# Graph attention on one core: the sender rows of four quads loaded row by row by SyncE instead of gathered by GpSimd

## The chip, the core and the metric

One core of a Trainium2 chip runs the whole kernel. The metric is the device time of one execution in microseconds, taken as the median of several runs; before the change it is 2042.45 us (three runs, 2042.1 to 2043.92). A profile of one further execution comes with it.

The engines are PE (TensorE; PEld is its loading of weights), DVE (VectorE), ACT (ScalarE), POOL (GpSimd) and SP (SyncE). SP computes nothing here; it issues DMAs and waits for semaphores.

## What is computed

There are N = 6250 nodes with 128 features `x`, and E = 206250 edges, sorted by receiver. Each edge has two vectors of 32 features, a weight, a sender and a receiver. Cut to what matters:

```python
w = silu(e1 @ rad_W1 + rad_b1) @ rad_W2 + rad_b2 + silu(e2 @ sph_W1 + sph_b1) @ sph_W2 + sph_b2
q = (x @ Wq)[dst];  k = (x @ Wk)[src];  v = (x @ Wv)[src]       # 8 heads of 16
alpha = (q * w * k).sum(head) / sqrt(16) * weight[:, None]
out = layernorm(x + segment_sum(alpha * v, dst, N) / 16)
```

So each edge needs one row of 256 numbers (k and v of its sender, 1 KB) from a table of all nodes. The senders come in no order.

## The kernel before

**Tiling.** 128 edges make a tile, four tiles a quad (512 edges, `QT = 4`), four quads a group. There are 403 quads and 101 groups; the last group has three quads. Everything is issued in an order written out by hand; no scheduler moves it.

**Head.** The kernel computes k and v for all nodes and stores them as `kv_tab` in DRAM (lines 223 to 236, 338 to 355). The senders of all edges are loaded to `src_i`, one column of 128 numbers for each tile. For the first ten quads (`XQ`) rows of `x` are gathered instead and k and v computed from them. Then come the gathers of four more quads (line 356), the sum of biases and the bias rows (358, 359), and the turning of the receivers on PE (360).

**Main loop** (lines 603 to 671). A step is a *slot*: one quad, taken in each group in the order 0, 2, 1, 3. The list `order` holds the quads in that order, and slot i works on `order[i]`. In a slot:

- PE computes the first layer of the quad two ahead (line 408), the queries at the edges of the quad one ahead (419), and that quad's second layer (455).
- ACT applies silu (440).
- DVE multiplies query and key of the quad one ahead (462, the first use of the quad's row of k and v), then by the edge's weight vector (469), sums the heads (471), and makes the message (484).
- PE adds the messages of the previous group by products with one-hot tables (495, 529).
- POOL gathers the rows of k and v for the quad 14 ahead (`AHEAD = RING - 2`): `gathers` makes a tile `kv` from a ring of 16 and issues four indirect DMAs, each of 128 rows (line 120). Each of them waits for one product of line 455 (its `marks`), so that no gather runs ahead of TensorE.
- SP loads, each once in a group, the window of `x` three groups ahead (`load_x`, lines 162 and 165; its address comes from a register loaded from `gb_i`), the features two groups ahead (142, 512 KB) and the receivers two groups ahead (153), and writes at most one finished window of rows in a slot (`write_rows`, 561). The loads of `x` and of the features wait for a product of TensorE.

The queues are in order: what SP is told in a slot waits until SP has issued all that stands before it.

After the loop the last quad is done in two halves, and the last rows are written (710). A general path for other receivers (lines 715 to 826) isn't taken.

Of the kernel before, what the change touches and what calls it, by code (L numbers as in the profile page):

```python
# [12 lines left out]
F32 = mybir.dt.float32  # L13
BF16 = mybir.dt.bfloat16
U8 = mybir.dt.uint8
I32 = mybir.dt.int32
AF = mybir.ActivationFunctionType
OP = mybir.AluOpType
# [3 lines left out]
SP = mybir.EngineType.SP  # L22
WAIT = mybir.DependencyInfo(mybir.DependencyClass.Sync, mybir.DependencyReason.DATA)

P = 128
N = 6250
D = 128
# [5 lines left out]
QT = 4  # L33
# [4 lines left out]
EQ = P * QT  # L38
# [3 lines left out]
ROWS = (NB + 1) * P  # L42
W = 32
LB = 4
XQ = 10
RING = 16
CHECK = 20
XL = 3
NEIGHBORS = 16.0
# [5 lines left out]
def gnn_kernel(ctx, tc, x, src, dst, weight, edges, rad_W1, rad_b1, rad_W2, rad_b2,  # L55
# [14 lines left out]
    nc = tc.nc  # L70
    const = ctx.enter_context(tc.tile_pool(name="const", bufs=1))
    dram = ctx.enter_context(tc.tile_pool(name="dram", bufs=1, space=DRAM))

    kv_tab = dram.tile([NB * P, 2 * D], F32, name="kv_tab")
# [5 lines left out]
    dst_i = const.tile([P, NT], I32, name="dst_i")  # L80
    src_i = const.tile([P, NT], I32, name="src_i")
    src_x = const.tile([P, math.ceil(XQ / NQ) * GT], I32, name="src_x")
    scale = const.tile([P, NT], F32, name="scale")
    w1 = const.tile([P, D], F32, name="w1")
    w2 = const.tile([P, 2, D], F32, name="w2")
# [5 lines left out]
    ident = const.tile([P, P], F32, name="ident")  # L91
# [24 lines left out]
    def quad_of(name, bufs, width=D):  # L116
        return ep.tile([P, QT, width], F32, name=name, bufs=bufs)

    def gather(o, table, index):
        return nc.gpsimd.indirect_dma_start(  # L120
            out=o, out_offset=None, in_=table,
            in_offset=bass.IndirectOffsetOnAxis(ap=index, axis=0))

    order = [g * NQ + j for g in range(NG) for j in (0, 2, 1, 3) if g * NQ + j < QUADS]
    r_of = {}
    feats_of, relb_of, act_of, kv_of, hot_of, hotT_of, x_of, q_of, msg_of = ({} for _ in range(9))
    po_of, part_of, to_of, tot_of, xT_of, y0_of, kq_of, pick_of, pq_of, pw_of = ({} for _ in range(10))

    def gathers(q, marks=()):

        kv = quad_of("kv", RING, 2 * D)
        for t in range(QT):
            o = gather(kv[:, t, :], kv_tab, src_i[:, q * QT + t:q * QT + t + 1])
            if marks:
                tc.add_manual_dep(o.ins, marks[t].ins.name, WAIT, reason="no gather ahead of TensorE")
        kv_of[q] = kv

    def load_feats(g, mark=None):  # L140
        feats_of[g] = gp.tile([P, EG // 2], F32, name="feats")
        o = nc.sync.dma_start(feats_of[g], edges[g])
        if mark is not None:
            tc.add_manual_dep(o.ins, mark.ins.name, WAIT, reason="one signal of TensorE a quad")
# [27 lines left out]

    nc.sync.dma_start(src_x, src[:, :math.ceil(XQ / NQ) * GT])
    nc.scalar.dma_start(wkv[:, :D], Wk)
# [12 lines left out]
    with tc.tile_pool(name="nodes", bufs=1) as nodes, \  # L187
            tc.tile_pool(name="nodes_ps", bufs=2, space=PSUM) as nps:
        chunks = [(c, min(QT, NB - c)) for c in range(0, NB, QT)]
        quads_x = order[:XQ]  # L190
        xs_of = {}
# [19 lines left out]
        def gather_x(q):  # L211
            xs_of[q, "x"] = xs = quad_of("msg", XQ)
            for t in range(QT):
                gather(xs[:, t, :], x, src_x[:, q * QT + t:q * QT + t + 1])
# [8 lines left out]
        def k_and_v(k, n):  # L223
            kvs = quad_of("kv", RING, 2 * D)
            for h in range(0, n, 2):
                m = min(2, n - h)
                pk = nps.tile([P, 2, 2 * D], F32, name="pk", bufs=3)
                for i in range(m):
                    nc.tensor.matmul(pk[:, i, :], xT_of[k][:, h + i, :], wkv, start=True, stop=True)
                nc.vector.tensor_copy(kvs[:, h:h + m, :], pk[:, :m, :])  # L230
            return kvs
# [88 lines left out]

        AHEAD = RING - 2
        beside = {3: [firsts], 4: [starts], 5: [lambda: receivers(0)], 6: [tables],
# [15 lines left out]
        for i, (k, n) in enumerate(work):  # L338
# [15 lines left out]
            if i == len(chunks) - 1:  # L354
                nc.sync.dma_start(scale, weight)
        for q in order[XQ:AHEAD]:
            gathers(q)
        nc.vector.tensor_tensor(bsum, b2[:, 0:1], b2[:, 1:2], op=OP.add)
        bias_rows()
        for t in range(P, NT, P):  # L360
# [5 lines left out]
    with tc.tile_pool(name="ps", bufs=1, space=PSUM) as pp:  # L366
# [113 lines left out]
        def messages(q, alpha, t=slice(0, QT), marks=()):  # L480

            if t.start == 0:
                msg_of[q] = quad_of("msg", XQ)
            o = nc.vector.tensor_tensor(  # L484
# [50 lines left out]
        def statistics(g):  # L535
            first = g // LB * LB if g < NG - 3 else g
            if g == first:
                y0_of[g] = (gp.tile([P, LB, D], F32, name="y0"), gp.tile([P, LB, 2], F32, name="mv"))
            y0, mv = y0_of[first]
# [4 lines left out]
            nc.vector.bn_aggr(mv[:, k - 1, :], st)  # L544
            if k == LB or g >= NG - 4:
                sd = gp.tile([P, LB], F32, name="sd")
                nc.scalar.activation(sd[:, :k], mv[:, :k, 1], AF.Sqrt, bias=eps)
                rs = gp.tile([P, LB], F32, name="rs")
                nc.vector.reciprocal(rs[:, :k], sd[:, :k])
                shift = gp.tile([P, LB], F32, name="shift")  # L550
                nc.vector.scalar_tensor_tensor(shift[:, :k], mv[:, :k, 0], -1.0, rs[:, :k],
# [6 lines left out]
        def write_rows(n=1):  # L558
            for _ in range(min(n, len(written))):
                g, y = written.pop(0)  # L560
                nc.sync.dma_start(rows_from(out, r_of.pop(g)), y.bitcast(U8))
# [41 lines left out]
        for g in range(NG):  # L603
            last = g == NG - 1
            for slot, j in enumerate((0, 2, 1, 3)):
                q = g * NQ + j
                i = g * NQ + slot
                if q >= QUADS:
                    continue
                turned, past, old = None, mark, marks  # L610
                if slot == 0 and g == CHECK + len(checks) + 1:
                    verdict()
                if slot == 0 and g + 1 < NG:
                    turned = turn_q(g + 1)
                if slot == 1 and 2 <= g:
                    turned = sum_group(g - 2)
                if slot == 2 and g + 1 < NG:
                    turned = make_q(g + 1)
                if 1 <= g:
                    for t in ((), (0, 1), (2, 3))[slot] if last else ((), (0, 1), (2,), (3,))[slot]:  # L620
                        mark = sum_quads(g - 1, t)
                if last and slot == 2:
                    po_of[g] = pp.tile([P, EQ], F32, name="ph", bufs=2)[:, :D]
                    for t in range(QT):
                        sum_wide(order[i - 2], t, start=(t == 0))
                if i + 2 < len(order):
                    first_layers(order[i + 2])
                if i + 1 < len(order):
                    mark = q_at_edges(order[i + 1])
                    marks = weigh(order[i + 1])  # L630
                if i + 2 < len(order):
                    silus(order[i + 2], mark, marks)
                if turned:
                    turned()
                if 1 <= g and slot == 3:
                    part_sums(g - 1)
                if i + AHEAD < len(order):
                    gathers(order[i + AHEAD], old[-QT:])
                if i + 1 < len(order):
                    multiply(order[i + 1], mark)  # L640
                    messages(q, scores(q, marks=marks), marks=marks)
                if slot == 0:
                    if g + XL < NG:
                        load_x(g + XL, past)
                if slot == 2 and g + 2 < NG:
                    load_feats(g + 2, past)
                    load_rel(g + 2)
                if slot == 1:
                    if g + 1 < NG:
                        one_hots_T(g + 1)  # L650
                    if g + 2 < NG:
                        pick(g + 2)
                    if 1 <= g < NG - 1:
                        place(g - 1)
                    if last:
                        wide_one_hots(g * NQ + 1)
                        place(g)
                        n = nc.values_load(general, min_val=0, max_val=1)
                if last and slot == 0:
                    wide_one_hots(g * NQ + 2)  # L660
                    place(g - 1)
                write_rows()
                if slot == (2 if last else 3) and 2 <= g:
                    statistics(g - 2)
                if slot == 3:
                    if g + 1 < NG - 1:
                        one_hots(g + 1)
                    if g + 1 == NG - 1:
                        wide_one_hots((g + 1) * NQ)
                    if CHECK <= g < CHECK + len(checks):  # L670
                        checks[g - CHECK]()
        g, q = NG - 1, order[-1]
# [18 lines left out]
        for t in range(QT // 2):  # L691
# [5 lines left out]
                                       op0=OP.mult, op1=OP.mult)  # L697
# [171 lines left out]
```

## Time and profile before

| | |
|---|---|
| median of 3 runs | 2042.45 us |
| profiled execution, its own time | 2043.99 us |
| its span, first to last instruction | 2042.2 us |
| mean granted clock of TensorE | 0.922 |
| PE busy / its weight loads | 90% / 75% of the span |
| DVE, ACT, POOL busy | 72%, 35%, 75% |
| DMA | 304 MB, 149 GB/s; mean share of the 16 DMA engines some 0.50 |
| queue of POOL's gathers | 76736 packets, 208.77 MB, 36.1% of 16 engines |
| queue of SP | 62912 packets, 92.00 MB, 13.8% |

The busy time of an engine counts its instructions alone. SP's instructions (register moves, semaphore waits, the issue of DMAs) don't count as busy, so its load is read from the duration and count of each kind. A group's line names the line of the kernel, the engine and operation, what is written from what, the count, then busy time in us and mean ns, and the idle time before it with what ended most of it. A wait is written as who waited, for whom, the sum in us, how often, and the longest.

### The profile page before, as it was taken

To read this page: it belongs to the slowest core of one execution; us is meant where nothing else is said; L and a number is where in the kernel's file an instruction comes from. 1 tells how busy PE (TensorE), PEld (TensorE's weight loads), DVE (VectorE), ACT (ScalarE), POOL (GpSimd) and SP (SyncE) were. 2 spreads that over 40 slices of the span, in tenths; PEclk is the share of its full clock that TensorE was granted. 3 is DMA by queue.
4 is the path that set the end of the run, shared out by engine and by line. 5 is a ranking of instruction groups with operands and counts; after the bars stand their busy time and mean duration, and the time that the engine had idled before them with its cause. 6 is when DMAs were issued, how large, how long until landed. Compare 5 with 4: busy or idle time off the path is not lost.

```text
span 2042.2 us, 44162 instructions
## 1 busy us (share of the span) xinstructions
PE 1843.1 (90%) x16011; PEld 1527.2 (75%) x16011; DVE 1466.9 (72%) x3005; ACT 720.1 (35%) x1425; POOL 1529.6 (75%) x1620
## 2 busy tenths in 40 slices
PE   9999998889899999898999989898998999898987
PEld 7788887777777777777777777777776777777776
DVE  6698887677767677677767667776766767677766
ACT  2334443333333323333333333233333333333333
POOL 7777777777777777777777777777777777777774
PEclk9899999899898898899888988998989989989889
DMA  8555554545445544545454554445454544544452
GB/s 309 149 150 154 154 157 145 153 136 152 140 147 141 153 146 142 146 143 152 136 151 142 149 148 145 146 142 148 140 152 136 153 140 148 151 143 147 140 149 81
DMA packets 141371, 304.03 MB, mean 149 GB/s; under 512 B 34028, under 2 KB 73820, under 8 KB 141148
## 3 DMA queue, kind: packets, MB, share of 16 engines
q0 software_dynamic: 76736, 208.77, 36.1%
q1 hardware_dynamic: 62912, 92.00, 13.8%
q8 instruction: 127, 2.08, 0.4%
q14 instruction: 96, 0.79, 0.1%
q10 hardware_dynamic: 1500, 0.40, 0.1%
HBM read 287.58 MB, written 13.46 MB: 147 GB/s over the span
## 4 chain that ended last, share of the span: by engine, by line
PE 50%; DMA 19%; DVE 14%; issue 7%; ACT 4%; POOL 4%; DVEq 0%; POOLq 0%; ACTq 0%
PE pw L455 24%; DMA kv<-kv_tab,src_i 19%; PE pq L419 10%; PE ph L408 7%; DVE kq L462 5%; PE po L495 4%; DVE side L471 2%; DVE kq L469 2%; PE pw L450 2%; POOL kv L120 2%; POOL msg L120 2%; ACT y L554 2%; ACT L440 2%; PE pq L388 1%; PE pq L529 1%
## 5 line engine op out<-in xcount | busy, mean ns | idle before, releaser
L120 POOL DMA_INDIRECT kv<-kv_tab,src_i x1572 | 1489.9, 948 | 479.7 <-issue 188.9
L440 ACT ACTIVATE act<-ph,b 128x512 f32<-128x512 f32 x806 | 518.7, 685 | 1176.6 <-PE pq L419 1149.0
L455 PE MATMUL pw<-w,act 128*128 128x128 f32 x6448 | 911.1, 300 | 0.1
L455 PEld LDWEIGHTS pw<-w,act 128*128 128x128 f32 x6448 | 830.1, 208 | 105.5 <-issue 93.2
L462 DVE TENSOR_TENSOR kq<-pq,kv 128x512 f32<-128x512 f32 x403 | 277.6, 689 | 401.6 <-DMA kv<-kv_tab,src_i 225.1
L419 PE MATMUL pq<-q,hotT 32*128 32x128 f32 x3224 | 498.1, 297 | 29.6 <-DVE kq L462 28.8
L408 PE MATMUL ph<-feats,w 32*128 32x512 f32 x1612 | 502.6, 681 | 23.3 <-ACT act L440 23.3
L419 PEld LDWEIGHTS pq<-q,hotT 32*128 32x128 f32 x3224 | 419.2, 199 | 87.0 <-issue 57.7
L471 DVE TENSOR_REDUCE side<-kq 128x32 f32<-128x512 f32 x404 | 279.9, 693 | 41.6
L484 DVE TENSOR_TENSOR msg<-kv,side 128x512 f32<-128x512 f32 x404 | 277.3, 686 | 43.4 <-DVE side L473 1.2
L469 DVE TENSOR_TENSOR kq<-pw,kq 128x512 f32<-128x512 f32 x404 | 274.1, 678 | 0.0
L408 PEld LDWEIGHTS ph<-feats,w 32*128 32x128 f32 x1612 | 137.6, 193 | 106.4 <-issue 59.6
L450 PE MATMUL pw<-brow,onesb 3*128 3x512 bf16 x403 | 161.1, 400 | 1.1 <-DVE kq L469 1.1
L495 PE MATMUL po<-msg,hot 128*32 128x128 f32 x3200 | 155.8, 292 | 0.0
L529 PE MATMUL pq<-part,to 128*128 128x128 f32 x200 | 45.6, 311 | 94.4 <-DVE kq L462 62.1
L473 DVE TENSOR_TENSOR side<-side,scale 128x32 f32<-128x32 f32 x404 | 80.6, 199 | 42.2 <-DVE side L471 0.5
L529 PEld LDWEIGHTS pq<-part,to 128*128 128x128 f32 x200 | 30.5, 192 | 106.8 <-issue 63.2
L495 PEld LDWEIGHTS po<-msg,hot 128*32 128x32 f32 x3200 | 71.4, 111 | 38.7 <-issue 5.3
L388 PE MATMUL pq<-wq,xT 128*128 128x128 f32 (+1 forms) x202 | 47.5, 320 | 37.3 <-DVE kq L462 36.9
L394 DVE TENSOR_TENSOR hotT<-relb,side 128x512 f32<-128x512 bf16 x101 | 68.7, 680 | 0.0
L388 PEld LDWEIGHTS pq<-wq,xT 128*128 128x128 f32 (+1 forms) x202 | 34.6, 214 | 45.6 <-DVE kq L462 44.9
L399 DVE TENSOR_TENSOR hot<-rel,side 128x512 f32<-128x512 f32 x100 | 66.1, 661 | 0.0
(107 smaller groups left out, 832.0 us busy)
## 6 DMA issues: line engine op xcount, KB each, us to landing
feats<-in_edges SPq DMA_DIRECT2D x101, 512.0 KB
kv<-kv_tab,src_i POOLq DMA_INDIRECT x1572
relb<-rel_lin SPq DMA_DIRECT2D x101, 128.0 KB
x<-in_x SPq DMA_DIRECT2D x101, 64.0 KB
out<-y SPq DMA_DIRECT2D x101, 64.0 KB
kv_tab<-kv SPq DMA_DIRECT2D x12, 512.0 KB
act<-in_x SPq DMA_DIRECT2D x12, 256.0 KB
dst_i<-in_dst SPq DMA_DIRECT2D x1, 808.0 KB
```

The costliest lines, as they stand in the source:

```text
L120: return nc.gpsimd.indirect_dma_start(out=o, out_offset=None, in_=table, in_offset=bass.IndirectOffsetOnAxis(ap=index, axis=0))
L388: nc.tensor.matmul(pt[:n, :D], xT_of[g][:, :n], wq, start=True, stop=True)
L408: return nc.tensor.matmul(act_of[q, i], w1[r0:r0 + R, :], feats_of[g][r0:r0 + R, c0:c0 + EQ], start=True, stop=True)
L419: o = nc.tensor.matmul(pq_of[q][:, t, :], hotT_of[g][b, t * P:(t + 1) * P], q_of[g][b, :], start=True, stop=True)
L440: o = nc.scalar.activation(act, act_of[q, i], AF.Silu, bias=b1[:, i:i + 1])
L450: nc.tensor.matmul(pw, onesb, brow.rearrange("p t d -> p (t d)"), start=True, stop=False)
L455: o = nc.tensor.matmul(pw[:, t, :], act_of[q, i][:, t * P:(t + 1) * P], w2[:, i, :], start=False, stop=(t == QT - 1 and i == 1))
L462: o = nc.vector.tensor_tensor(kq_of[q], pq_of[q], kv_of[q][:, :, :D], op=OP.mult)
L469: nc.vector.tensor_tensor(m, pw_of[q][:, t, :], m, op=OP.mult)
L471: o = nc.vector.tensor_reduce(alpha, m.rearrange("p t (h e) -> p t h e", e=HD), AX.X, OP.add)
L484: o = nc.vector.tensor_tensor(msg_of[q][:, t, :].rearrange("p t (h e) -> p t h e", e=HD), kv_of[q][:, t, D:].rearrange("p t (h e) -> p t h ...
L495: o = nc.tensor.matmul(po_of[g][j * W:(j + 1) * W, :], hot_of[g][:, j * QT + t, :], msg_of[g * NQ + j][:, t, :], start=(t == 0), stop=(t = ...
```

## The change

Four quads are not gathered any more. With `ROW_LEAD = 8`, `every` is (403 - 8) // 4 = 98, so `row_at` is 98, 196, 294, 392: the quads at these positions of `order`. For them `gathers` returns at once.

Their rows come from SP. `load_rows(i)`, called in every slot after `write_rows`, issues units of 16 edges: one load of 16 addresses into registers of SP, then 16 DMAs, each of one row of 1 KB from `kv_tab` to one partition of a tile `rows` (two buffers). A quad has 32 units. They are spread over the slots since the last such quad's (91 slots for the first, 98 for each other), none or one in a slot, and end eight slots before the quad's own position.

The addresses are made at the head: DVE multiplies the senders of the four quads by 1024, PE turns the 128x16 result, DVE copies it to `at_i` as integers, so that the addresses of one tile lie in one partition.

The change's short description also speaks of small weights on SyncE's queue; the diff has no such edit, and the small weights are still issued by ACT (line 343).

```diff
+ROW_BYTES = 2 * D * 4
+ROW_QUADS = 4
+ROW_LEAD = 8
+ROW_UNIT = 16
...
+    at_i = const.tile([ROW_QUADS * QT, P], I32, name="at_i")
...
+    every = (len(order) - ROW_LEAD) // ROW_QUADS
+    row_at = [(n + 1) * every for n in range(ROW_QUADS)]
+    row_quads = {order[i] for i in row_at}
...
     def gathers(q, marks=()):
 
+        if q in row_quads:
+            return
         kv = quad_of("kv", RING, 2 * D)
...
+    def load_rows(i):
+
+        k = max(i + ROW_LEAD - 1, 0) // every
+        if k >= ROW_QUADS:
+            return
+        q, start = order[row_at[k]], max(k * every - ROW_LEAD + 1, 0)
+        slots, units = row_at[k] - ROW_LEAD + 1 - start, EQ // ROW_UNIT
+        a, b = ((j * units + slots - 1) // slots for j in (i - start, i - start + 1))
+        if i == start:
+            kv_of[q] = quad_of("rows", 2, 2 * D)
+        table = kv_tab.bitcast(U8).rearrange("(o n) b -> o (n b)", o=1)
+        for u in range(a, min(b, units)):
+            t, e = u * ROW_UNIT // P, u * ROW_UNIT % P
+            _, rows = nc.values_load_multi_w_load_instructions(
+                at_i[k * QT + t:k * QT + t + 1, e:e + ROW_UNIT], engines=(SP,), min_val=0,
+                max_val=(N - 1) * ROW_BYTES, skip_runtime_bounds_check_because="senders are nodes")
+            for p in range(ROW_UNIT):
+                nc.sync.dma_start(kv_of[q][e + p:e + p + 1, t, :].bitcast(U8),
+                                  table[:, ds(rows[p], ROW_BYTES)])
...
         for q in order[XQ:AHEAD]:
             gathers(q)
+        rows_f = nodes.tile([P, ROW_QUADS * QT], F32, name="rows_f")
+        for k, i in enumerate(row_at):
+            nc.vector.tensor_scalar(rows_f[:, k * QT:(k + 1) * QT],
+                                    src_i[:, order[i] * QT:(order[i] + 1) * QT],
+                                    float(ROW_BYTES), None, op0=OP.mult)
+        pt = nps.tile([P, QT, P], F32, name="pt", bufs=3)
+        nc.tensor.transpose(pt[:ROW_QUADS * QT, 0, :], rows_f, ident)
+        nc.vector.tensor_copy(at_i, pt[:ROW_QUADS * QT, 0, :])
         nc.vector.tensor_tensor(bsum, b2[:, 0:1], b2[:, 1:2], op=OP.add)
         bias_rows()
...
                 write_rows()
+                load_rows(i)
                 if slot == (2 if last else 3) and 2 <= g:
```

## The prediction

> **What bounds the kernel now.** I read the page's busy times first, then the groups of instructions, the timeline of POOL, the waits, and the count of multiplications (line 462, one for each quad of 512 edges) by stage.
>
> ```profile
> PE 1843.1 (90%) x16011; PEld 1527.2 (75%) x16011; DVE 1466.9 (72%) x3005; ACT 720.1 (35%) x1425; POOL 1529.6 (75%) x1620
> ...
> L120 POOL DMA_INDIRECT kv<-kv_tab,src_i x1572 | 1489.9, 948 | 479.7 <-issue 188.9
> ```
>
> By busy share PE looks like the bound and POOL like an engine with a quarter of its time to spare. The second line takes that back: 1489.9 us busy and 479.7 us idle make 1969.6 us for 1572 gathers, 1.253 us each. POOL's timeline shows what the idle time is:
>
> ```profile
> 2017.20 0.94 POOL L120 DMA_INDIRECT kv<-kv_tab,src_i  x1 [0.30 <-PE pw L455]
> ...
> 2018.45 0.94 POOL L120 DMA_INDIRECT kv<-kv_tab,src_i  x1 [0.30 <-issue]
> ...
> 2019.70 0.95 POOL L120 DMA_INDIRECT kv<-kv_tab,src_i  x1 [0.31 <-issue]
> ...
> 2020.95 0.94 POOL L120 DMA_INDIRECT kv<-kv_tab,src_i  x1 [0.30 <-issue]
> ...
> 2022.20 0.95 POOL L120 DMA_INDIRECT kv<-kv_tab,src_i  x1 [0.31 <-issue]
> ```
>
> The gap is 0.30 us whatever is named as its cause: a fixed step of the instruction, not a wait. From 53.76 us to 2023.15 us POOL gathers without a pause, 4 x 1.253 = 5.01 us a quad. What the others would do, the stages show (length, busy time and count of line 462, then clock, DMA share, GB/s):
>
> ```profile
> 100.00:150.00 50.00, 9.31 (x14) 1.00 0.52 154
> 150.00:200.00 50.00, 8.22 (x12) 0.97 0.54 155
> 200.00:250.00 50.00, 8.23 (x12) 0.97 0.53 154
> 250.00:300.00 50.00, 8.90 (x13) 1.00 0.51 151
> ...
> 600.00:800.00 200.00, 27.57 (x40) 0.88 0.50 146
> ```
>
> While the ring of rows is full (to about 300 us) 51 quads take 200 us, 3.92 us each, with PE 96 to 100% busy; later 40 take 200 us, 5.0 us each, which is POOL's pace. The waits agree: hardly any on a gather's DMA before 300 us, and over the whole span
>
> ```profile
> DVE kq L462 <- DMA kv<-kv_tab,src_i: 225.1, 165, 4.7
> ```
>
> So POOL sets the end: its last gather, then 19.1 us of tail. PE, at 3.9 to 4.2 us a quad, has about a fifth to spare.
>
> **What goes.** Four quads (positions 98, 196, 294 and 392 of 403) lose their four gathers: 16 x 1.253 = 20.05 us off POOL, with nothing beside them. After each of these quads PE and DVE have two quads to do in one 5.01 us gap; at some 4.1 us each they fall 3.2 us behind and recover 0.9 us a quad, four quads later. Even the last has ten quads left for that, so all four count. What is late next is still the next gather.
>
> **What comes at the head.** Four multiplications 128x4, a transpose on PE and a copy stand before the bias rows. Nearest rows: a tensor-scalar 128x4 takes 0.23 us (line 504), and small ones start 0.07 to 0.2 us apart; a transpose 0.34 us (line 307); a copy of 128x128 0.29 us (line 296). That is 0.5 + 0.34 + 0.25 and two hand-overs of about 0.1, or 1.3 us. It isn't hidden: PE's first product of the main loop starts at 65.78 us, after the pick of 65.40 us, which follows the bias rows on DVE; and the first gather that waits for TensorE (75.26 us) stood idle 0.89 us instead of 0.30, so it already waits for that chain. I take 1.3 us, lost once; bounds 0 (another wait covers it) and 2.5 us (each step at its longest row, and the twelve turns of the receivers pushed back behind the new transpose).
>
> **What comes on SP.** 2048 row loads of 1 KB in 128 units: one register load for 16 addresses, then 16 DMAs. The rows nearest to it:
>
> ```profile
> L162 SPq TENSOR_LOAD <-gb_i x101: 269/737/1132, 23.8 to 1944.2; - x101
> ```
>
> ```profile
> L165 SPq MOVE x<-in_x x101: 29/38/39, 24.9 to 1945.1; - x101
> L165 SPq DMA_DIRECT2D x<-in_x x101: 332/339/358, 25.0 to 1952.0; - x101
> L165 SPq EVENT_SEMAPHORE  x97: 17/17/28, 68.5 to 1945.0; - x97
> ```
>
> A DMA whose address is in a register costs 0.339 + 0.038 + 0.017 = 0.394 us of SP, 16 of them 6.3 us (8.8 us if back to back they take 0.497, the longest of line 205's loads of x). The load of 16 registers isn't in the trace: 0.74 us if it costs what one register does, 11.8 us if it costs 16 times the median. I take 16 times the fastest, 0.269, so 4.3 us, as consecutive reads should not each bear the median's full delay. A unit is then 10.6 us, with ends at 7.0 and 20.6.
>
> The Trainium skill ("Runtime: NRT & Kernel Launch", "What's in a NEFF") puts a register load at about 200 ns a register even in bulk; by that estimate the load is 3.2 us, the unit 9.5 us, and the sum stays what it is.
>
> The units lie on slots 0 to 384, one in 3.01 slots (2.84 for the first quad), that is 14.2 to 15.1 us at POOL's pace. SP's own work in four slots is 0.74 + 0.34 (x) + 0.34 (features) + 0.57 (receivers) + 0.34 (rows out) + 0.1 = 2.43 us, so 1.8 us in that stretch. This leaves 12.5 us or more for a unit of 10.6: SP is filled to about 85%, and its present waits for PE (over 1300 us in all) cover it. Behind a unit on SP stand the features and receivers of two groups ahead and the rows out. They come up to 10.6 us later than now, and have about four slots, 20 us, less some 5 us to land. The rows themselves must be there seven slots (35 us) after the last unit.
>
> SP also waits for older DMAs, because their signals are shared:
>
> ```profile
> SPq L334 <- DMA wkv<-in_Wv: 0.6, 1, 0.6
> ```
>
> That load has no data in common with the one named. Between them stand seven other loads from SP and ACT, so I read eight signals in turn: a row waits until the eighth DMA before it has landed. A gather lands 1.92 us after POOL has written it (ended 2013.13, used 2015.05), and eight rows take 3.2 us to issue, so it costs nothing, unless a landing takes over 3.2 us, as behind a 512 KB feature load (the rows out wait for the one before up to 5.7 us). DVE's multiplication of such a quad must see up to eight signals: well under 1 us, in an engine 72% busy.
>
> **The sum.** 20.05 - 1.3 = 18.75 us off. The profiled execution took 2043.99 us (span 2042.2), 1.54 us over the median of 2042.45; it would become 2025.2, and the median 2023.7. Everything else I cost at nothing: the 2 MB travel either way, the tail is the same.
>
> **Rivals.**
> 1. *Part is given back* (2029.9 us). The two quads in one gap are not caught up after the last of the four (PE's clock falls to 0.86 in some stretches): 5.0 us lost, and the head costs 2.5: 2042.45 - 20.05 + 7.5. For it: line 455 at times takes 3.71 us for 16 products instead of 2.05. Against it: ten quads remain.
> 2. *SP becomes the bound* (slower). It decides once a unit takes over 12.5 us, which with 6.3 us of DMAs is a register load over 6.2 us, 0.39 us a register. Then features arrive late for every group, and SP's order paces the loop. At 0.50 us a register (the register loads of line 658 take 0.46 to 0.54) a unit is 14.3 us: 70 us head, 128 x 14.3 + 96 x 2.43 = 2064, 18 quads at 5.0 and 16 us tail make 2240 us; at the median 0.737 it is 2730. For it: only single loads are seen, and their median is above the limit. Against it: one instruction for 16 neighbouring words should not pay 16 times.
> 3. *No gain* (2043.7 us). The transfers, not POOL's writing of descriptors, pace the gathers; then it is the same who issues them, and the head's 1.3 us remain. For it: 19% of the chain of waits is put down to the gathers' DMA. Against it: a DMA share of 0.50 in every stage, and POOL's even steps. The Trainium skill ("DMA: Bandwidth & Descriptors", "Issuing engines are not separate DMA queues") states this rule: all queues run on the same 16 engines, and another issuing engine saves only the sequencer's time to initiate, usually small. By it the change would be worth nothing; the trace has that time as 1.253 us a gather on the path, so here it is not small.
>
> **How the numbers follow.** Forecast 70%, rival 1 12%, rival 2 14%, rival 3 4%. The forecast's own spread is 2020.5 (head 0, and POOL's few long gathers, up to 1.82 us, fewer) to 2027. The range 2020.5 to 2034 takes in the forecast and rival 1 (82%). What a measurement tells from no change is about 0.2%, 4.1 us: faster 0.82, same 0.04, slower 0.14.
>
> **What would show it.** Right: 1556 gathers of kv, still 0.30 us apart, the last ending near 2004.5; line 462 waiting for gathers as now and not for rows; 128 register loads of under 6 us. The head: the first gather with a long wait begins near 76.6. Wrong: POOL idle for more than 0.3 us in the loop, PE waiting for features, or SP without waits for PE (rival 2); a POOL that ends 19 us earlier with a longer tail (rival 1).

## The result and the profile after

The changed kernel takes 2025.62 us (median of six runs, 2023.26 to 2026.46) against 2042.51 us before (six runs). The two medians are 16.9 us apart (0.83%). The ratio over all runs is 0.9913, or 0.87% faster, with a 95% interval of 0.9903 to 0.9923, which is 15.7 to 19.8 us. The profiled execution took 2025.53 us, its span is 2023.8 us. In two of the sessions below (four runs) the kernel before itself took 2602.8 and 2602.6 us instead of 2043, at a granted clock near 0.81, so their numbers stand only against that.

The page after has the same two lines as before, and they say the same thing: a busy PE, and a POOL whose idle time is no wait but part of each gather's step.

```profile
PE 1832.9 (91%) x16012; PEld 1526.1 (75%) x16012; DVE 1469.2 (73%) x3010; ACT 718.9 (36%) x1425; POOL 1511.9 (75%) x1604
...
L125 POOL DMA_INDIRECT kv<-kv_tab,src_i x1556 | 1472.5, 946 | 476.6 <-issue 184.3
```

There are 16 gathers fewer, and 1472.5 us busy and 476.6 us idle for 1556 are 1.253 us each, as before. POOL's timeline ends 20.3 us earlier (2022.20 us before) with the same gaps:

```profile
1999.36 0.95 POOL L125 DMA_INDIRECT kv<-kv_tab,src_i  x1 [0.31 <-issue]
2000.61 0.95 POOL L125 DMA_INDIRECT kv<-kv_tab,src_i  x1 [0.30 <-issue]
2001.86 0.95 POOL L125 DMA_INDIRECT kv<-kv_tab,src_i  x1 [0.30 <-issue]
```

The multiplication (now line 500) by stage, in the columns of before, shows the two paces again. While the ring of rows is full, 51 quads take 200 us, 3.92 us each. Later 39 take 200 us, 5.1 us each, about POOL's pace of 5.0:

```profile
100.00:150.00 50.00, 9.25 (x14) 1.00 0.57 164
150.00:200.00 50.00, 7.91 (x12) 0.93 0.54 157
200.00:250.00 50.00, 8.24 (x12) 0.97 0.52 156
250.00:300.00 50.00, 8.92 (x13) 1.00 0.53 154
600.00:800.00 200.00, 26.91 (x39) 0.91 0.50 147
```

It still waits for gathers, hardly less than before, and never for loaded rows, which no line of the waits names there:

```profile
DVE kq L500 <- DMA kv<-kv_tab,src_i: 216.3, 145, 3.7
```

What SP does for it is now in the trace (count, then shortest, median and longest ns): the load of 16 registers, and each row's move and issue. These are the answers for line 163 and for line 167.

```profile
L163 SPq TENSOR_LOAD <-at_i x128: 973/1161/1532, 78.5 to 1901.7; - x128
```

```profile
L167 SPq MOVE rows<-kv_tab x2048: 29/29/38, 79.5 to 1908.1; - x187
L167 SPq DMA_DIRECT2D rows<-kv_tab x2048: 224/228/352, 80.0 to 1908.2; - x187
```

On SP's timeline the sixteen rows of a unit mostly take 5.2 to 6.4 us, so with its register load a unit is 6.4 to 7.6 us. SP's waits for PE (features, line 172, and `x`, line 195) fall from 1331 us to 481:

```profile
SPq L172 <- PE pw L493: 215.8, 76, 10.8
...
SPq L195 <- PE pq L457: 165.4, 34, 8.4
...
SPq L172 <- PE pq L457: 84.3, 17, 11.1
SPq L167 <- DMA relb<-rel_lin: 59.3, 56, 1.7
...
SPq L195 <- PE pw L493: 15.3, 28, 7.3
```

In the line of 59.3 us rows wait for loads of receivers, with which they share no data. That fits the prediction's reading that DMAs take their signals in turn.

**Where the 18.4 us of the two spans lie.** From the first gather that waits for TensorE to the last gather, POOL makes 1539 steps in 1924.68 us after and 1555 in 1946.94 before, so 22.3 us less: 20.0 for sixteen steps, and 2.2 because a step is 1.4 ns shorter on the mean. The long gathers are not the reason: in these stretches eight take over 1.00 us after, two before. The mean step of the single executions kept here scatters by as much whatever the kernel: 1.2521 us before, 1.2506 after, 1.2514 with the head alone and 1.2502 with unused loads (both below). So the 2.2 us are not shown to be the change's. The first of these gathers starts 1.92 us later. From the last gather's start to the end it takes 21.94 us instead of 20.00. That is -22.3 + 1.9 + 1.9.

### The profile page after: what moved, and what is told of

It is laid out like the page before. It is cut to its first block, busy times and chain, and to the rows that moved or that the text cites. A ratio compares the mean times of both kernels' runs of the same rounds, so it can differ in the third digit from the quotient of the medians.

```text
span 2023.8 us, 48401 instructions
## 1 busy us (share of the span) xinstructions
PE 1832.9 (91%) x16012; PEld 1526.1 (75%) x16012; DVE 1469.2 (73%) x3010; ACT 718.9 (36%) x1425; POOL 1511.9 (75%) x1604
## 4 chain that ended last, share of the span: by engine, by line
PE 51%; DMA 21%; DVE 12%; issue 7%; ACT 4%; POOL 4%; DVEq 0%; POOLq 0%; ACTq 0%
PE pw L493 25%; DMA kv<-kv_tab,src_i 20%; PE pq L457 10%; PE ph L446 7%; DVE kq L500 5%; PE po L533 3%; PE pw L488 2%; POOL kv L125 2%; DVE side L509 2%; DVE kq L507 2%; POOL msg L125 2%; ACT y L592 1%; ACT L478 1%; PE pq L567 1%; PE pq L426 1%
## 5 line engine op out<-in xcount | busy, mean ns | idle before, releaser
L125 POOL DMA_INDIRECT kv<-kv_tab,src_i x1556 | 1472.5, 946 | 476.6 <-issue 184.3
L522 DVE TENSOR_TENSOR msg<-kv,side 128x512 f32<-128x512 f32 (+1 forms) x400 | 274.8, 687 | 42.9 <-DVE side L511 1.8
```

What stands on the lines that cost most here:

```text
L125: return nc.gpsimd.indirect_dma_start(out=o, out_offset=None, in_=table, in_offset=bass.IndirectOffsetOnAxis(ap=index, axis=0))
L522: o = nc.vector.tensor_tensor(msg_of[q][:, t, :].rearrange("p t (h e) -> p t h e", e=HD), kv_of[q][:, t, D:].rearrange("p t (h e) -> p t h ...
```

## The experiments

| run | what differs from the change | median | ratio to before, 95% |
|---|---|---|---|
| e1_head_only | addresses made, all quads gathered, no rows loaded | 2046.0 | 1.0014, 1.0004 to 1.0023 |
| e2_rows_unused | all quads gathered, rows loaded and not used | 2046.1 | 1.0015, 1.0006 to 1.0024 |
| e3_no_loads | neither gathered nor loaded, the four quads take other rows | 2027.1 | 0.9917, 0.9903 to 0.9931 |
| e4_head_early | addresses made earlier | 2025.3 | 0.9914, 0.9900 to 0.9928 |
| e8_single_quiet | one register load a row | 2445.1 | 1.197, 1.193 to 1.201 |
| e9_quads6_quiet | six quads | 2017.2 | 0.9873, 0.9856 to 0.9889 |
| e10_quads8_quiet | eight quads | 2264.8 | 1.109, 1.107 to 1.110 |
| e11_quads7_early | seven quads, addresses earlier | 2066.5 | 1.0123, 1.0106 to 1.0140 |
| e5, e6, e7, e12 | e8's edit; six quads; eight; six, addresses earlier; the kernel before at 2602.8, in e12 2602.6 | 2618.8, 2634.5, 2679.9, 2634.6 | 1.0071, 1.0123, 1.0305, 1.0131 |

My theory was that POOL's step of 1.253 us a gather sets the time, that SP's loads are hidden while SP keeps up, and that the head is lost once. The rivals were a cost of the loads themselves, and SP as the bound.

### The head alone, the loads alone, and the loads left out

```diff
 e1 and e2: def gathers
-        if q in row_quads:
-            return
 e1 and e3: main loop
-                load_rows(i)
 e2: load_rows writes its rows to a tile that nobody reads
-            kv_of[q] = quad_of("rows", 2, 2 * D)
+            spare_of[q] = quad_of("rows", 2, 2 * D)
...
 e3: def gathers
         if q in row_quads:
+            kv_of[q] = kv_of[order[order.index(q) - 1]]
             return
```

Expected of the head alone: 

> The head of the change alone: the addresses are made, but all 403 quads are gathered and SyncE loads no rows. Theory A (POOL's pace sets the time; the head delays the first gather that waits for TensorE and is lost once): slower than before by the wait seen after the change, 2.77 us instead of 0.89, so by 1.5 to 2 us, 2044.2 us. Rival B (the head is covered, and the 1.9 us missing from the forecast belong to SyncE's loads): 2042.5 us. Rival C (they belong to the end of the kernel, where the last write landed later): 2042.5 us with a head wait under 1 us, or 2044.2 with the tail, not the head, longer.

Expected of the loads without their use: 

> Head and row loads as in the change, but all 403 quads are gathered too and the loaded rows are not used: SyncE's loads without their benefit. Theory A: the loads lie beside everything, so the time is that of the head alone, 2044.2 us, and POOL makes 1572 gathers 0.30 us apart. Rival B (the loads slow the gathers or delay features and receivers): 2 us or more above the head alone, 2046 us or over.

Expected without the loads: 

> The four quads are neither gathered nor loaded: they are computed with the rows of the quad before them, so the output differs there. Everything else as after the change, the head too. Theory A: SyncE's 2048 loads cost nothing, so the time is that of the change, 2025.6 us. Rival B: the loads cost some 2 us, so 2023.6 us here.

The head alone is slower by 0.14%, 2.9 us in the medians (0.8 to 4.7 by the interval), and its trace has the wait that was seen after the change. The lines are from before, from after, from the head alone and from the run without loads:

```profile
75.26 0.95 POOL L120 DMA_INDIRECT kv<-kv_tab,src_i  x1 [0.89 <-PE pw L455]
```

```profile
77.18 0.94 POOL L125 DMA_INDIRECT kv<-kv_tab,src_i  x1 [2.77 <-PE pw L493]
```

```profile
76.90 0.94 POOL L125 DMA_INDIRECT kv<-kv_tab,src_i  x1 [2.78 <-PE pw L491]
```

```profile
79.05 0.95 POOL L125 DMA_INDIRECT kv<-kv_tab,src_i  x1 [4.57 <-PE pw L494]
```

Not all of the 2.9 us need be the head's. In that execution the first such gather starts 1.64 us later than before, and the stretch from the last gather's start to the end takes 22.5 us instead of 20.0.

The 2048 loads put on top of this cost nothing: 2046.1 beside 2046.0 us, ratio 1.0015 beside 1.0014. Nor is anything won by leaving them out: 0.9917 beside the change's 0.9913. The intervals leave room for some 2 us either way, and the run without loads lost 1.9 us more than the change before its first waiting gather. The head alone and the run without loads differ in the sixteen gathers, and their medians by 18.9 us; sixteen steps are 20.0. So the gain is that of POOL's sixteen steps, and the loads lie beside the rest.

### The head moved

```diff
+        def row_addresses():           # the multiplications, the transpose and the copy
...
             if i >= len(chunks):
                 kv_of[k[0]] = kvs
+                if i == len(chunks) + 6:
+                    row_addresses()
...
-        rows_f = nodes.tile([P, ROW_QUADS * QT], F32, name="rows_f")      # the old place
...
```

Expected: 

> The change with its head moved: the addresses are made among the first ten quads, where DVE and TensorE wait for gathers of x, not ahead of the bias rows. Theory A: the head's delay goes, the first gather that waits for TensorE stands idle 0.9 us again, and the time is 1.5 to 2 us under the change: 2023.8 us. Rivals B and C: 2025.6 us as before.

The first gather that waits for TensorE then starts at 75.81 us (idle 1.52 us), 1.4 us earlier than after the change. The time shows no gain: 0.9914 beside 0.9913, where 1.4 us would be 0.0007. That fits the addresses as the cause of most of the added wait, but it is one execution against one, and the 4.57 us above show that this wait can differ by 1.8 us with the same head. Whether its time can be had back is too small a question for these intervals.

### The price of a register load

```diff
-            _, rows = nc.values_load_multi_w_load_instructions(...16 addresses...)
             for p in range(ROW_UNIT):
+                row_at_p = nc.values_load(...address p...)
                 nc.sync.dma_start(kv_of[q][e + p:e + p + 1, t, :].bitcast(U8),
-                                  table[:, ds(rows[p], ROW_BYTES)])
+                                  table[:, ds(row_at_p, ROW_BYTES)])
```

Expected, first run: 

> The change with one register load for each row instead of one for 16, so 2048 register loads. It sets the price of SyncE's unit above the point (12.5 us) at which the prediction's second rival decides: 16 times a load of 0.74 us, a move and an issue of 0.23 to 0.34 are 16 to 18 us. Theory (SyncE paces the loop beyond that point): 70 + 128 x 16 to 18 + 96 x 2.43 + 106 us, so about 2450 to 2710 us, features and receivers late, POOL waiting. Rival (SyncE's work is hidden whatever it costs, or single loads are cheaper in a row, 0.27 us): 2026 us as the change.

That run took 2618.8 us beside 2602.8 us of the kernel before, 1.0071 of it, and so tells nothing of SP's price beside 2043 us.

Expected, second run: 

> One register load for each row again, on a quiet chip: the first time the kernel before itself took 2602.8 us beside it, so that run says nothing of SyncE's price. There a row took 0.93 us of SyncE (a single load 0.50, issue 0.26, moves and gaps), so a unit of 16 is 14.9 us, over the 12.5 us at which the prediction's second rival decides. Theory (beyond that point SyncE paces the loop): 70 + 128 x 14.9 + 96 x 2.43 + 106 = 2316 us, features or receivers late, POOL idle. Rival (SyncE's work is hidden whatever it costs): 2026 us.

It took 2445.1 us (two runs), a fifth more than before. The trace shows SP as the bound, by who waits for what:

```profile
DVE hotT L432 <- DMA relb<-rel_lin: 609.1, 77, 17.3
POOL kv L125 <- PE pw L493: 541.0, 587, 13.1
PE ph L446 <- DMA feats<-in_edges: 529.9, 68, 16.6
...
DVE kq L500 <- DMA kv<-kv_tab,src_i: 17.1, 17, 2.9
```

In the change, features and receivers are no line of this list at all; here PE and DVE wait for them up to 17 us, POOL waits for PE, and the multiplication scarcely waits for gathers any more. A single load takes 0.50 us (median 504 ns of 2048), sixteen rows 14.0 us. The 2316 us expected were 129 too few. The sum held none of SP's waits for older writes of rows out, and they are the largest wait that SP has left,

```profile
SPq L599 <- DMA out<-y: 114.2, 48, 5.8
```

which I had taken to vanish once SP is late. That they make up the 129 us was not tried.

### More quads, until SP is full

```diff
-ROW_QUADS = 4
+ROW_QUADS = 6        (7, 8)
```

Expected of six and of eight, first runs: 

> Six quads loaded by SyncE instead of four. A unit takes about 7 us of SyncE in the trace after the change (register load 1.16, sixteen rows 5.2 to 6.4); six quads leave it one unit in 2.03 slots, 10.2 us less 1.2 us of its other work. Theory (each gather off POOL is worth 1.25 us while SyncE keeps up): 24 gathers, 30.0 us less than before, plus the head's 1.6: 2014 us. Rival (SyncE's share of two thirds already delays it, or TensorE is the bound by now): no less than 2020 us.

> Eight quads loaded by SyncE. A unit comes every 1.53 slots (1.31 ahead of the first), 7.7 us (6.6) at POOL's pace, and SyncE's other work is 0.9 us of that; a unit took 6.6 to 7.6 us in the trace after the change. Theory (SyncE is at its limit here): it fills, its waits for TensorE vanish, features come late, and the time is SyncE's: about 70 + 256 x 7.1 + 245 + 20 = 2150 us, more than before. Rival (the waits inside a unit shrink under load, 5.5 us a unit, and it still fits): 32 gathers less, 2042.5 - 40.0 + 1.6 = 2004 us.

Beside 2602.8 us of the kernel before they cost 1.2% and 3.1%. Expected of the second runs, and of seven with the early head: 

> Six quads by SyncE, again on a quiet chip. A unit takes 6.4 to 7.6 us and has 9 us. Theory (each gather off POOL is worth 1.25 us while SyncE keeps up): 24 gathers, 30.0 us less than before, plus 1.6 to 2.9 of the head: 2014 to 2015.5 us. Rival (SyncE's lateness shows by now): 2020 us or more.

> Eight quads by SyncE, again on a quiet chip. A unit takes 6.4 to 7.6 us and has 6.7 us (5.8 ahead of the first of the eight). Theory (SyncE is just beyond its limit): its waits for TensorE go, features or receivers come late, and the time is SyncE's: 70 + 256 x 7.0 + 96 x 2.43 + 106 = 2201 us at most; with units of 6.4, 2048. Rival (still hidden): 32 gathers less, 2004 us.

> Seven quads by SyncE with the addresses made early, among the first ten quads: a candidate to beat the change. A unit has 7.7 us (6.7 ahead of the first) and takes 6.4 to 7.6. Theory: 28 gathers less, 2042.5 - 35.0 + 0.5 = 2008 us. Rival (SyncE fills at the first of the seven quads and delays features there): 2010 to 2030 us.

Six quads take 2017.2 us, 25.9 less than before, against 30.0 for 24 gathers. Seven are 1.2% slower than before, eight 11%. The waits for receivers and features grow step by step, from none with four quads to 40 and 24 us with six, 263 and 195 with seven, 448 and 342 with eight. First six quads, then eight:

```profile
DVE hotT L432 <- DMA relb<-rel_lin: 40.2, 15, 8.2
...
PE ph L446 <- DMA feats<-in_edges: 24.1, 9, 7.3
```

```profile
DVE hotT L432 <- DMA relb<-rel_lin: 448.2, 81, 9.7
...
POOL kv L125 <- PE pw L493: 392.3, 612, 9.1
...
PE ph L446 <- DMA feats<-in_edges: 341.8, 75, 8.6
```

With six, the trace shows where the missing time lies: not in late features. No gather after the first that waits stands idle over 0.35 us, so POOL still paces the loop. Its profiled execution (2022.4 us, the slowest of the four) has a span 21.5 us under that of before. Against the 30.0 us stand a head wait of 4.55 us, which starts the gathers 3.6 us later than before, steps of 1.2537 us on the mean instead of 1.2521 (2.6 us), and an end 2.4 us longer. The run without loads had the same head wait (4.57 us), so neither SP's units nor the two more quads need be its cause; what it is stays open. For seven I expected 2008 us, POOL's pace, and got 2066.5: there SP's units of 6.4 to 7.6 us had 7.7, and 6.7 ahead of the first, which, by the late features and receivers, was not enough. For eight I expected at most 2201 and got 2264.8. That sum again left out SP's waits for rows out, which are 61 us there. Between six and seven quads, then, the gain turns into a loss; I had put SP's limit at eight.

Six quads with the early head were the candidate for the best: 

> Six quads by SyncE with the addresses made early, among the first ten quads: a candidate to beat the change. With six quads and the head in its place the first gather that waits for TensorE stood idle 4.55 us; with the early head of four quads 1.52 us. Theory (POOL's pace sets the time and what it loses at the head is lost): 2.5 to 3 us under the six quads of before, so 2014.3 us against a kernel before of 2043. Rival (the head's loss is made good later, since SyncE's lateness takes the place of POOL's pace in some stretches): 2017 us, no better.

It took 1.0131 of the 2602.6 us of the kernel before, as six quads did without it beside 2602.8 (1.0123). This is POOL's line in that run:

```profile
L125 POOL DMA_INDIRECT kv<-kv_tab,src_i x1548 | 1464.8, 946 | 1044.1 <-PE pw L497 431.1
```

POOL stood idle 1044 us there instead of 477, so its steps did not set that time, and whether the early head beats plain six quads is open. Six quads (0.9873, interval to 0.9889) beat the change (0.9913, from 0.9903), and both beat the kernel before.

## Why the prediction was right, point by point

- **POOL as the bound** (forecast 20.05 us for 16 gathers): right. POOL's steps are unchanged, 22.3 us go from its stretch, and e1 to e3 show that the gain comes with the gathers and not with anything SP does. Sixteen steps of these are 20.0; the other 2.2 lie within the scatter of the mean step and were not forecast.
- **PE and DVE catch up after each of the four quads**: right. The last multiplication starts 3.2 us after the last gather's start, both before (2022.20, 2025.36) and after (2001.86, 2005.07). After the quads whose multiplication starts at 503.11, 989.07, 1472.79 and 1958.29 us, the multiplication first waits for a gather again at 519.06, 1006.12, 1515.99 and 1994.68. That is four quads later for the first two, as forecast, but nine and eight for the others. After the last only two quads were left, so the margin was thinner than the six that the forecast left. The prediction's sign for its first rival, a POOL that ends 19 us earlier with a longer tail, did appear (20.3 us, and 1.9 us longer), but the tail's growth lies behind the last DVE instruction (see the sum), not in quads that were late.
- **The head**: 1.3 us expected. The first product of the loop moved from 65.78 to 67.08 us, which is 1.3 (0.2 of it stands already at the first gather of `kv`, ahead of the address work); but the gathers moved by 1.92 us. The 0.6 between them is two pairs of products that took 0.77 and 0.80 us instead of 0.46 and 0.49: the granted clock was 0.50 there (67.0 to 69.1 us) against 0.95 before (65.7 to 67.2). Why is open. With the early head (e4) the pairs start at 65.71 us, as before the change, and run at 0.50 as well, so their later place is not the reason.
- **SP's unit**: 10.6 us taken, ends 7.0 and 20.6; measured 6.4 to 7.6, so at and below the lower end. The register load was the mis-sized term, 1.16 us instead of 4.3, and the issue of one row takes 228 ns, not the 339 of a window of 128 rows. Some 200 ns a register, as the Trainium skill has it ("Runtime: NRT & Kernel Launch", "Instruction fetch mechanics", which is the section that states it, not the one that the prediction names), would be 3.2 us by estimate. The measured load is 1.16 us for sixteen, and 0.50 us for one in e8, so here the measurement decides. Nothing in the sum hung on it.
- **SP as the bound** (the second rival, from 12.5 us a unit on): did not come, since the unit is far below, and it exists: with a unit of expected 14.9 us, above the 12.5, e8 lost 20%. The formula for its time was 129 us short there.
- **No gain, since the transfers pace** (third rival): not so here. The Trainium skill's rule ("DMA: Bandwidth & Descriptors", "Issuing engines are not separate DMA queues") is that another issuing engine saves only the time to initiate a DMA, usually small; by these runs that time was the path, 1.25 us a gather.
- **The sum**: 18.75 us forecast, 16.9 measured in the medians. The forecast is a ratio of 0.9908, which lies inside the measured interval, so the medians can't tell the 1.9 us between them from scatter. The two profiled executions differ by 18.5 us, 0.3 less than forecast, and that closeness is in part luck: steps shorter on the mean gave 2.2 us that the sum did not hold, and 0.6 us more at the head and 1.9 us at the end took them back. The tail, which the prediction costed at nothing because it is the same, is the term that was furthest off in these two. Its 1.9 us lie between the last DVE instruction and SP's drain, its last wait for the writes: 2.7 us before, 4.5 after. The loads are not the reason, since the same stretch is 4.6 us with the head alone, 4.1 with unused loads, 3.0 without loads and 4.2 with the early head. Whether it varies from one execution to the next, or the head's work has a part in it, one trace of each kernel doesn't show.

## What to carry to other kernels

An engine that is 75% busy can be the bound: divide its whole stretch by its instructions, and look whether its gaps are all alike, before you believe a page's busy shares. Work taken from such an engine is worth its full step, and may cost the receiving engine many times as much, as long as that one waits anyway: a quad is 5.0 us of POOL and 32 units of 6.4 to 7.6 us of SP. Price the receiver's slack with its remaining waits included: here six quads still paid, and with seven the gain had turned into a loss, as the features and receivers that SP issues behind the rows came late.

## What the runs showed of the hardware

- A load of 16 neighbouring addresses into registers of SP took 1.16 us (median of 128), one of a single address 0.50 us (e8, median of 2048): some 44 ns for each further register, by estimate from the two.
- The issue of a one-row load from a register address took 228 ns on SP (median of 2048), that of a window of 128 rows 339 ns before the change and 359 after it.
- A gather of 128 rows of 1 KB took POOL 0.95 us and a gap of 0.30 us ahead of it, before and after the change, whatever was named as the gap's cause.
